# A mixture-of-experts stage whose scatters add straight into the output, with a bound on the row number

## The chip, the cores and the metric

The kernel runs on one core of one Trainium2 chip. TensorE (PE), VectorE (DVE), ScalarE (ACT), GpSimd (POOL) and SyncE (SP) each run their own list of instructions in order and wait for one another on semaphores; 16 DMA engines move data between the core's SBUF and HBM, fed from queues that SP, ACT and POOL issue to. The metric is the device time of one execution in microseconds (us), lower is better. A change is judged by runs of both kernels on the same chip.

## The reference, cut to what matters

One layer over 512 tokens of width 512: cross-attention over 8192 context rows, a Mamba block with an MLP, and a mixture of experts with a shared expert. Each part adds to `x`. The change is in the last part:

```python
logits = jnp.einsum('btc,ec->bte', x, router_w)
top_vals, top_idx = jax.lax.top_k(logits, 2)
gates = jax.nn.sigmoid(top_vals)
w_full = jnp.zeros((N, 16)).at[jnp.arange(N)[:, None], top_idx].add(gates)
gate, up = jnp.split(jnp.einsum('nc,ech->neh', xf, gate_up_w), 2, axis=-1)
out_all = jnp.einsum('neh,ehc->nec', jax.nn.silu(gate) * up, down_w)
moe = jnp.einsum('ne,nec->nc', w_full, out_all)
...
return moe + shared
...
x = x + ffn(layernorm(x), ...)
```

Each of the 512 tokens goes to 2 of 16 experts, so there are 1024 pairs of token and expert. The kernel computes only these. With the inputs of the reference the router sends 27, 19, 24, 112, 116, 16, 61, 45, 28, 72, 36, 46, 53, 165, 142 and 62 tokens to experts 0 to 15.

## The kernel before, in words

The attention takes the first 1.8 ms or so, the Mamba block and its MLP most of the rest, the experts the last 0.18 ms. Only the last part is touched.

**Sorting the tokens.** Tokens are sorted into blocks of 128 slots: blocks 0 to 15 are the experts' own, blocks 16 to 22 take what an expert has above 128. A slot is a row of `xd_d` in HBM: the normed token in two fp16 halves, the number of the row that its result goes to, and its gate. Early in the kernel (`weight_prep`, L512 on) every slot is filled with zeros and the row number 512 + p for partition p, an address behind the 512 tokens. `route` (L1240) then writes the 1024 real slots over it with eight scatters. A block's filled slots are its lowest, since tokens are numbered within their expert; the empty ones keep the row numbers 512 to 639.

**The sum.** `sum_d` (L66) is a scratch tensor in HBM with 512 + 128 rows of 512 fp32 values; the last 128 are the dump for empty slots, zeroed at L524. When the residual `x_sb` with the shared expert's result is ready, POOL copies it to the first 512 rows (L1416). Each block's result is then added to the rows its slots name. At the end SP copies the 512 rows to the output (L1425).

**The experts' loop** is `moe` (L1363). Blocks 0 to 17 always run (`16 + MOV`, MOV = 2); blocks 18 to 22 only where `total`, the number of extra blocks in use, is above 2 (L1421). For each block k:

- SP loads the weights in pieces of 512 KB (`piece`, L1135: `wef`), six of one expert; ACT makes the fp16 high half (L1148), DVE the low half (L1149). Twenty gate/up pieces are ready before the loop starts.
- `moe_load` (L1300) loads block k + 3 into a tile `xd` (6 buffers): the first three from POOL's queue, the others from ACT's.
- TensorE transposes the block's tokens (L1315), ACT copies them out (L1401, `xk`), TensorE multiplies by gate and up (L1328), ACT and DVE do silu and the product (L1336 to L1341), TensorE multiplies the block before by its down weights (L1349).
- `moe_out` (L1355) scales the result by the gate on ACT (L1357, `myo`) and issues the scatter on POOL (L1358): one instruction that adds 128 rows of 2 KB into rows of HBM, given by the list `row`, which lies in the block's `xd` tile.

Two blocks may hold the same token, so a scatter waits until the one before it has landed; the tile framework sets this wait, as it does for every tensor that is written twice. The same framework makes a load into a reused `xd` buffer wait until the scatter that reads the row list in it has landed. ACT issues that load in order with its other work, so ACT waits too.

On POOL's queue in this stage are, in order: the eight scatters of `route`, three loads of `xd`, the copy of L1416 and the 18 scatters. On SP's queue are the weights and, last, the copy of L1425.

Of the kernel before, what the change touches and what calls it, by code (L numbers as in the profile page):

```python
# [9 lines left out]
F32 = mybir.dt.float32  # L10
U16 = mybir.dt.uint16
AF = mybir.ActivationFunctionType
ALU = mybir.AluOpType
# [4 lines left out]
P = 128  # L18
NQ = 512
DM = 512  # L20
# [21 lines left out]
def perceiver_layer(ctx: ExitStack, tc: tile.TileContext, a: dict, out: bass.AP):  # L42
    nc = tc.nc

    const = ctx.enter_context(tc.tile_pool(name="const", bufs=1))
    scr = ctx.enter_context(tc.tile_pool(name="scr", bufs=1, space=DRAM))
# [3 lines left out]
    x_sb = const.tile([P, 4, DM], F32, name="x_sb")  # L50
# [12 lines left out]
        for n, k in (("inp", 8), ("outp", 4), ("w1", 8), ("w3", 8), ("w2", 8), ("rsg", 4), ("rsu", 4), ("rsd", 4), ("Wo", 4))  # L63
    }

    sum_d = scr.tile([NQ + P, DM], F32, name="sum_d")  # L66
    xd_d = scr.tile([(16 + NOV) * P, XR], U16, name="xd_d")

    def norm_stats(pool, src, tag):
# [442 lines left out]
    def weight_prep():  # L512
        zero = sb2.tile([P, 2 * DM], F16, name="zero", tag="t2k", bufs=4)
        nc.gpsimd.memset(zero, 0.0)
        none = sb2.tile([P, 2, 1], mybir.dt.int32, name="none", bufs=1)
        nc.gpsimd.memset(none, 0)
        nc.gpsimd.iota(none[:, 0], pattern=[[0, 1]], base=NQ, channel_multiplier=1)
        for k in range(16 + NOV):
            rows = slice(k * P, (k + 1) * P)
            nc.sync.dma_start(xd_d[rows, 0 : 2 * DM], zero.bitcast(U16))  # L520
            nc.sync.dma_start(xd_d[rows, 2 * DM : XR], none.rearrange("p a o -> p (a o)").bitcast(U16))
            if k % 4 == 3 or k == 15 + NOV:
                yield
        nc.sync.dma_start(sum_d[NQ : NQ + P, :], zero.bitcast(F32))  # L524
        blocks = [(name, i, dst) for name in mlp_d for i, dst in enumerate(mlp_d[name])]

        def fetch(j):
            f = sb2.tile([P, 1024], F32, name="mpf", bufs=2)
            nc.sync.dma_start(f, a[blocks[j][0]][:, blocks[j][1]])
            return f  # L530

        nf = fetch(0)
        yield
        for j, (name, i, dst) in enumerate(blocks):
            f = nf
            if j + 1 < len(blocks):
                nf = fetch(j + 1)
            yield
            for h in range(2):
                sl = slice(h * 512, h * 512 + 512)  # L540
                hl = sb2.tile([P, 2, 512], F16, name="mph", tag="t2k", bufs=4)
                nc.vector.tensor_scalar(hl[:, 0], f[:, sl], WF, None, ALU.mult)
                nc.vector.scalar_tensor_tensor(hl[:, 1], f[:, sl], WF, hl[:, 0], ALU.mult, ALU.subtract)
                nc.sync.dma_start(dst[:, :, sl], hl)
                yield
# [20 lines left out]
    advance(start + LEAD)  # L566
    load(1)
    pend, enders, early = [], [], weight_prep()
    NFILL = 12 * NSTEP - 6
    rate = ((NPASS - 1) * PASSN + LAST - LEAD) / NFILL  # L570
# [44 lines left out]
    for m in range(NSTEP):  # L615
        n = NLAST * NSTEP + m
        if m % 4 == 0:
            load(n // 4 + 1)
        cur = scores(u, m, loads[n // 4], sp, True)
        while len(pend) > 1:  # L620
            drain()
        pend.append((u, m, cur))
        if m == 0:
            tl = tail(tc, a, out, const, scr, ident, x_sb, mlp_d, oT, sum_d, xd_d, (ps_s, ps_o, ps_x, bank_j))
        for _ in range(2):
            if m >= 1 and not ready:
                ready = next(tl)
# [12 lines left out]
def tail(tc, a, out, const, scr, ident, x_sb, mlp_d, oT, sum_d, xd_d, psums):  # L640
    nc = tc.nc
# [493 lines left out]
    def piece(k, t, i):  # L1135
# [23 lines left out]
        out=lt, in_=lt, pattern=[[1, P]], compare_op=ALU.is_gt, fill=0.0, base=0, channel_multiplier=-1  # L1159
# [195 lines left out]
    def moe_out(py, row, gate_):  # L1355
        yo = g2.tile([P, DM], F32, name="myo", tag="yo", bufs=4)
        nc.scalar.activation(yo, py, AF.Copy, scale=gate_)  # L1357
        nc.gpsimd.indirect_dma_start(  # L1358
            out=sum_d[:], out_offset=bass.IndirectOffsetOnAxis(ap=row, axis=0), in_=yo, in_offset=None,
            compute_op=ALU.add,  # L1360
        )

    def moe(ks, ready):  # L1363

        last = ks[-1]
        todo = [(k, i) for k in ks for i in range(4)][ready:]
        each = len(todo) // (len(ks) - 1)
        free = [NWE - ready]  # L1370

        def split(n):
            n = min(n, len(todo), free[0])
            free[0] -= n
            for _ in range(n):
                k, i = todo.pop(0)
                piece(k, "gu", i)
            return n

        lastk[0] = last  # L1380
        for k in range(ks[0], ks[0] + 3):
            moe_load(k, nc.gpsimd)
        piece(ks[0], "dn", 0)
        xin_ = moe_in(ks[0])
        nc.scalar.copy(xin_[0], xin_[1])
        prev, out_ = None, None
        for k in ks:
            if out_:
                moe_out(*out_)
                out_ = None  # L1390
            piece(k, "dn", 1)
            n = split(each)
            xk, _, *to = xin_
            mid = moe_mid(*moe_up(k, xk))
            free[0] += NC4
            if k < last:
                xin_ = moe_in(k + 1)
            next(mid)
            moe_load(k + 3, nc.scalar)
            if k < last:  # L1400
                nc.scalar.copy(xin_[0], xin_[1])  # L1401
            gg = next(mid)
            split(each - n)
            while (k + 1, "gu", 3) not in W and k < last:
                split(1)
            if k < last:
                piece(k + 1, "dn", 0)
            if prev:
                out_ = moe_down(*prev[0:2]), *prev[2]
            prev = k, gg, to  # L1410
        if out_:
            moe_out(*out_)
        moe_out(moe_down(*prev[0:2]), *prev[2])

    regs = [nc.sync.value_load(oii[0:1, k : k + 1], min_val=0, max_val=15) for k in range(NOV)]
    nc.gpsimd.dma_start(sum_d[0:NQ].rearrange("(p i) d -> p i d", i=4), x_sb)  # L1416
    assert next(pre, None) is None
    moe(range(16 + MOV), NWE)
    mo.close()
# [1 line left out]
    with tc.If(total > MOV):  # L1421
        for n in range(4):
            piece(16 + MOV, "gu", n)
        moe(range(16 + MOV, 16 + NOV), 4)
    nc.sync.dma_start(out, sum_d[0:NQ].rearrange("(p i) d -> p i d", i=4))  # L1425
    es.close()


# [66 lines left out]
```

## Time and profile before

| | us |
|---|---|
| median of 3 runs (lowest, highest) | 2570.77 (2567.15, 2572.27) |
| the profiled execution | 2565.43 |
| its span, first to last instruction | 2563.7 |
| TensorE busy in the span | 2361.3 (92%) |
| POOL busy in the span | 73.8 (3%) |
| first scatter of the experts starts at | 2404.55 |
| last scatter of the experts starts at | 2551.43 |
| granted TensorE clock, mean | 0.979 |

The span is cut into 40 slices of 64 us, and each digit is the busy share in tenths. The experts' stage is the last three slices: there the DMA engines are as busy as at any time, and POOL, idle for most of the kernel, has its scatters.

```profile
PE   7999899999999999999999998998878678899896
POOL 3000000000000000000000000000000000001112
DMA  7983777787777787777778664777711212388897
```

The stage by itself, in stretches: busy time of each engine with the number of instructions, then granted clock, share of the 16 DMA engines and GB/s.

```profile
2404.00:2440.00 36.00, 31.63 (x416) 25.11 (x414) 28.58 (x29) 29.07 (x36) 8.85 (x4) 1.00 1.00 348
2440.00:2470.00 30.00, 29.74 (x425) 25.05 (x422) 25.29 (x25) 26.47 (x33) 5.52 (x3) 1.00 1.03 361
2470.00:2500.00 30.00, 28.93 (x375) 22.78 (x373) 24.65 (x25) 23.59 (x29) 4.80 (x3) 1.00 1.03 354
2500.00:2530.00 30.00, 28.17 (x400) 23.76 (x399) 23.37 (x23) 25.98 (x32) 6.49 (x4) 1.00 1.02 364
2530.00:2564.00 34.00, 16.28 (x189) 11.78 (x186) 10.89 (x11) 10.99 (x15) 7.46 (x4) 0.78 0.48 111
```

The columns of engines are PE, PEld (weight load, beside PE), DVE, ACT and POOL. In the middle stretches all but POOL are busy for most of the time and the DMA is full; in the last one the weights have all arrived and little but scatters is left.

### The profile page before, as it was taken

To read this page: it belongs to the slowest core of one execution; us is meant where nothing else is said; L and a number is where in the kernel's file an instruction comes from. 1 tells how busy PE (TensorE), PEld (TensorE's weight loads), DVE (VectorE), ACT (ScalarE), POOL (GpSimd) and SP (SyncE) were. 2 spreads that over 40 slices of the span, in tenths; PEclk is the share of its full clock that TensorE was granted. 3 is DMA by queue.
4 is the path that set the end of the run, shared out by engine and by line. 5 is a ranking of instruction groups with operands and counts; after the bars stand their busy time and mean duration, and the time that the engine had idled before them with its cause. 6 is when DMAs were issued, how large, how long until landed. Compare 5 with 4: busy or idle time off the path is not lost. (4 is left out here: it accounts for less than half of the span.)

```text
span 2563.7 us, 56681 instructions
## 1 busy us (share of the span) xinstructions
PE 2361.3 (92%) x22958; PEld 1722.3 (67%) x22958; DVE 2046.2 (80%) x2378; ACT 1947.5 (76%) x3734; POOL 73.8 (3%) x77
## 2 busy tenths in 40 slices
PE   7999899999999999999999998998878678899896
PEld 3555577777666777766777776897756456577775
DVE  6776578888888888887888777998899999746685
ACT  5787788888878888877888888997958557434685
POOL 3000000000000000000000000000000000001112
PEclk9999999999999999999999999999999889999998
DMA  7983777787777787777778664777711212388897
GB/s 267 304 272 133 215 213 227 231 238 232 216 231 227 219 247 236 226 213 213 240 216 234 175 171 133 196 207 210 200 59 40 101 50 84 125 281 274 315 360 232
DMA packets 355199, 529.52 MB, mean 207 GB/s; under 512 B 28194, under 2 KB 221922, under 8 KB 354660
## 3 DMA queue, kind: packets, MB, share of 16 engines
q1 hardware_dynamic: 349156, 513.23, 65.7%
q0 software_dynamic: 3616, 8.66, 1.5%
q8 instruction: 182, 2.98, 0.5%
q10 hardware_dynamic: 2160, 3.95, 0.5%
q14 instruction: 85, 0.70, 0.1%
HBM read 396.65 MB, written 126.97 MB: 204 GB/s over the span
## 5 line engine op out<-in xcount | busy, mean ns | idle before, releaser
L380 DVE TENSOR_TENSOR phl<-p,phl 128x1024 f16<-128x1024 f32 x512 | 626.8, 1225 | 191.5 <-ACT phl L377 175.6
L375 ACT ACTIVATE p<-pss 128x512 f32<-128x512 f32 x1024 | 597.6, 622 | 112.1 <-issue 43.5
L308 ACT ACTIVATE sf<-psx 128x512 f16<-128x512 f32 x1024 | 558.6, 625 | 70.2 <-PE psx L303 69.5
L367 PE MATMUL pss<-qhh,k 128*128 128x256 f16 x2048 | 478.3, 274 | 14.1 <-ACT phl L377 11.9
L368 PE MATMUL pss<-qlm,kb 128*128 128x256 f16 x2048 | 477.1, 273 | 0.8 <-DMA v<-v_d 0.7
L316 DVE TENSOR_TENSOR runm<-runm,sf 128x2048 f16<-128x2048 f16 x240 | 292.4, 1220 | 51.4 <-ACT sf L308 51.3
L397 PE MATMUL po<-v,phl 128*128 128x130 f16 x4096 | 322.3, 220 | 3.9 <-DVE oq L410 3.4
L377 ACT ACTIVATE phl<-pss 128x512 f16<-128x512 f32 x512 | 312.8, 611 | 0.0
L397 PEld LDWEIGHTS <-phl 128*128 128x128 f16 x4096 | 270.5, 98 | 61.7 <-issue 15.3
L278 PE MATMUL psv<-wh_v,ctxc 128*128 128x256 f16 x1024 | 283.4, 277 | 7.3 <-ACT wh_v L179 3.2
L279 PE MATMUL psv<-wl_v,ctxc 128*128 128x256 f16 x1024 | 282.0, 275 | 1.1 <-DVE wl_v L180 1.1
L280 PE MATMUL psv<-wh_v,ctxc 128*128 128x256 f16 x1024 | 282.0, 275 | 0.0
L367 PEld LDWEIGHTS <-k 128*128 128x128 f16 x2048 | 200.3, 98 | 65.0 <-issue 20.0
L368 PEld LDWEIGHTS <-kb 128*128 128x128 f16 x2048 | 200.7, 98 | 52.1 <-issue 14.9
L303 PE MATMUL psx<-khl,qh 64*128 64x512 f16 x1024 | 208.1, 386 | 18.2 <-ACT sf L308 13.1
L929 PE MATMUL py<-hs,ident 128*128 128x256 f32 x512 | 141.2, 430 | 76.6 <-DVE hs L926 76.5
L400 PE MATMUL po<-v,phl 128*128 128x65 f16 x4096 | 208.2, 193 | 1.4 <-DVE phl L380 1.4
L254 PE MATMUL psk<-ctxc,wh_k 128*128 128x512 f16 x512 | 197.4, 386 | 10.8 <-ACT ctxc L237 9.0
L379 DVE CAST phl<-p 128x1024 f16<-128x1024 f32 x256 | 176.1, 688 | 30.8 <-ACT p L375 30.6
L255 PE MATMUL psk<-ctxc,wh_k 128*128 128x512 f16 x512 | 196.0, 383 | 0.9 <-DVE ctxc L238 0.9
L256 PE MATMUL psk<-ctxc,wl_k 128*128 128x512 f16 x512 | 195.9, 383 | 0.0
L929 PEld LDWEIGHTS py<-hs,ident 128*128 128x128 f32 x512 | 104.8, 213 | 108.3 <-DVE hs L926 90.9
(315 smaller groups left out, 3814.4 us busy)
## 6 DMA issues: line engine op xcount, KB each, us to landing
v<-v_d SPq DMA_DIRECT2D x128, 520.0 KB
k<-k_d SPq DMA_DIRECT2D x256, 256.0 KB
ctxc<-ctx_d SPq DMA_DIRECT2D x96, 512.0 KB
wef<-in_gu_dram SPq DMA_DIRECT2D x72, 512.0 KB
v_d<-vs SPq DMA_DIRECT2D x128, 260.0 KB
k_d<-khl SPq DMA_DIRECT2D x128, 256.0 KB
kb<-k_d SPq DMA_DIRECT2D x128, 256.0 KB
wpm<-w_d SPq DMA_DIRECT2D x48, 512.0 KB
```

The costliest lines, as they stand in the source:

```text
L278: nc.tensor.matmul(ps[:, t, :], lhsT=ct[i // 2][:, 0, i % 2, sl], rhs=wh[:, i, :], start=i == 0, stop=False)
L279: nc.tensor.matmul(ps[:, t, :], lhsT=ct[i // 2][:, 0, i % 2, sl], rhs=wl[:, i, :], start=False, stop=False)
L280: nc.tensor.matmul(ps[:, t, :], lhsT=ct[i // 2][:, 1, i % 2, sl], rhs=wh[:, i, :], start=False, stop=i == NC4 - 1)
L308: nc.scalar.activation(dst, ps, AF.Copy, scale=1.0 / (8.0 * WS))
L316: nc.vector.tensor_tensor(r, r, sf, ALU.max)
L367: nc.tensor.matmul(ps[:, hh], lhsT=k[:, hh, sl], rhs=qhh[:, hh, qs], start=True, stop=False)
L368: nc.tensor.matmul(ps[:, hh], lhsT=b[:, hh, sl], rhs=qlm[:, hh, qs], start=False, stop=True)
L375: nc.scalar.activation(p32[:, i], pss[i], AF.Exp, scale=sc)
L377: nc.scalar.activation(ph[:, i], pss[i], AF.Exp, scale=sc)
L380: nc.vector.tensor_tensor(pl, p32, ph, ALU.subtract)
L397: nc.tensor.matmul(o, lhsT=ph[:, i, hh, qs], rhs=vv, start=first, stop=False, **kw)
L929: nc.tensor.matmul(py[:, j, :], lhsT=ident, rhs=hs[:, n, 1:], start=k == 0, stop=False)
```

## The change

The scratch tensor `sum_d` goes; its name now stands for the output, seen as 512 rows. The zeroing of its dump rows goes, and the copy at the end. The scatter gets a bound, `NQ - 1` = 511, with `oob_is_err=False`: a row number above it is no error, and its row is left out. The slots' row numbers are as before, so an empty slot still says 512 + p.

```diff
-    sum_d = scr.tile([NQ + P, DM], F32, name="sum_d")
+    sum_d = out.rearrange("p i d -> (p i) d")
...
-        nc.sync.dma_start(sum_d[NQ : NQ + P, :], zero.bitcast(F32))
...
         nc.gpsimd.indirect_dma_start(
-            out=sum_d[:], out_offset=bass.IndirectOffsetOnAxis(ap=row, axis=0), in_=yo, in_offset=None,
-            compute_op=ALU.add,
+            out=sum_d, out_offset=bass.IndirectOffsetOnAxis(ap=row, axis=0), in_=yo, in_offset=None,
+            bounds_check=NQ - 1, oob_is_err=False, compute_op=ALU.add,
         )
...
-    nc.gpsimd.dma_start(sum_d[0:NQ].rearrange("(p i) d -> p i d", i=4), x_sb)
+    nc.gpsimd.dma_start(out, x_sb)
...
-    nc.sync.dma_start(out, sum_d[0:NQ].rearrange("(p i) d -> p i d", i=4))
```

The row number of a token is 4p + i for partition p and column i of `x_sb`, in the scratch tensor as in the output, so the numbers that the slots carry stay right.

## The prediction

> **What bounds the kernel now.** I read the chain that ended last first, then the scatters in order of time, then one stretch of the timeline with every engine, then the DMA queues of that stretch, and last the waits at the end.
>
> ```profile
> 2545.94 1.55 DMA sum_d<-myo,xd
> 2547.49 3.74 issue
> 2551.22 0.49 POOLq L1420
> 2551.72 1.26 POOL sum_d L1358
> ```
>
> The chain ends in scatters (L1358): one lands, the next goes out. The whole list of scatters shows how far back this reaches. Scatter 0 starts at 2404.55, scatter 17 at 2551.43: 17 gaps, 8.64 us each on average. The tile view gives the landing (start to last byte) as 4.8 least, 8.0 median, 10.2 most.
>
> ```profile
> 2472.88 1.55 POOL L1358 DMA_INDIRECT sum_d<-myo,xd  x1 [7.26 <-issue]
> 2475.00 0.68 ACT L1357 ACTIVATE myo<-acc,xd 128x512 f32<-128x512 f32 x1
> ...
> 2481.62 0.33 ACTq L1300 DMA_DIRECT2D xd<-xd_d  x1
> 2481.99 1.01 ACT L1401 COPY xk<-pxd 128x1024 f16<-128x1024 f16 x1 [2.04 <-DMA sum_d<-myo,xd]
> 2482.26 1.55 POOL L1358 DMA_INDIRECT sum_d<-myo,xd  x1 [7.83 <-issue]
> ```
>
> Columns: start, duration, engine and line; in brackets the idle time before. The next `myo` is ready at 2475.68, yet its scatter starts at 2482.26: it waits for the scatter of 2472.88, whose rows it may share. ACT waits for the same landing at L1300, because the new `xd` takes the buffer (one of 6) whose row list that scatter still reads. From that release to the next scatter's start 0.64 us pass (2481.62 to 2482.26; the same at 2463.43, 2489.74, 2499.91, 2507.89 and 2517.34). So a gap is landing + 0.64, and 17 x (8.0 + 0.64) = 146.9, exactly the 146.88 from first to last: every gap is set by a landing. `myo` is ahead of its scatter by 0.28 us at scatter 0, 7.1 at scatter 10, 4.4 at scatter 17.
>
> TensorE is close behind. Its cycle per expert, from transposes to transposes (L1315), is 8.39 where nothing waits (2426.45 to 2434.84, 2444.30 to 2452.69). Over the 14 cycles from 2405.38 to 2532.54 the excess over 8.39 is 127.16 - 117.46 = 9.7 us; the five cycles in which L1300 came late (2463 to 2527) hold 3.8 of it, weights most of the rest. And the DMA engines are full (2463 to 2475):
>
> ```profile
> q1 hardware_dynamic: 1078, 3.92, 83.9%
> q0 software_dynamic: 144, 0.26, 12.0%
> ```
>
> q0 is a single scatter: 144 packets, which I read as 128 rows and 16 completions, 0.26 MB and 12% of 16 engines. Alone, without weights beside it, a scatter lands in 4.8.
>
> The end, by SP's and POOL's own waits:
>
> ```profile
> 2551.43 1.55 POOL L1358 DMA_INDIRECT sum_d<-myo,xd  x1 [3.94 <-issue]
> 2557.31 0.59 SPq L1425 DMA_DIRECT2D out_dram<-sum_d  x1
> ...
> SPq L1425 <- DMA sum_d<-myo,xd: 20.1, 1, 20.1
> SPq L1490 <- DMA out_dram<-sum_d: 4.2, 1, 4.2
> ...
> L1490 POOLq DRAIN  x1: 2520/2520/2520, 2557.3 to 2557.3; - x1
> ```
>
> POOL's last wait for scatter 17 ends at 2556.4, SP is let go at 2557.25, the copy of 1 MB is issued and lands by 2562.4, the closing barrier ends at 2563.7.
>
> **The end copy, removed.** SP stood still for nothing else, and nothing is queued behind it. Without it SP would be at its closing waits at 2557.3, but POOL's drain runs from 2557.3 to 2559.8, and the barrier needs it. If the drain stays, 2562.4 - 2559.8 = 2.6 us are saved; if it was held up by the copy, 2562.4 - 2557.3 = 5.1. I take 2.6: the copy is SP's, not POOL's.
>
> **Edits at nothing.** The zeroing of the dump rows (L524) is one 256 KB issue of 0.45 us on SP at 293.9; SP's next issue is at 303.5 and TensorE, VectorE and ScalarE are at 0.7 to 0.9 there; uncovered it would be 0.45. L1416 writes the same 1 MB from the same queue to another tensor; issued at 2379.91, landed in 5.9, it is over 18 us before scatter 0. The order among copy and scatters now hangs on the output tensor; I take it to be kept, wait for wait, with the same things queued behind (POOL has only scatters; ACT's stall at L1300 as before).
>
> **The bound: what it costs.** No row shows a scatter with a bound. The check is POOL work for 128 rows. The plain scatter L1240 takes 0.96 us at least, the adding one 1.54: one more duty on each row costs 0.58. The slowest adding scatter took 2.63, 1.1 more than the fastest. So 0 to +1.1 a scatter; I take +0.2, a third of the 0.58, as a bare comparison sends no second transfer.
>
> **The bound: what it saves.** 18 blocks of 128 slots are 2304 rows, of which 512 x 2 = 1024 are filled: 1280 rows (56%) are dropped, 2 KB read, added and written each. Lower bound: nothing, if each dropped row still makes a transfer or the slowest engine keeps its rows. Upper bound: a plain load of 257 KB (`xd<-xd_d`) lands in 3.9 in the same traffic, so at most 8.0 - 3.9 = 4.1 of a landing belongs to the rows, and 56% is 2.3. I take 1.0, under half, because filled slots are the low partitions and need not leave all engines alike. Net landing: -0.8 (bounds -2.3 and +1.1). At the end, without traffic, the rows' part is at most 4.8 - 3.4 (the quickest `xd` load) = 1.4; the last two blocks hold 37 and 14 rows by the router, so -1.0 and -1.25, +0.2 each.
>
> The Trainium skill, "DMA: Bandwidth & Descriptors", section "Anatomy of one DMA — SWDGE (gpsimd) path", fits 2.0 us plus bytes over 436 GB/s: 2.6 for this scatter, where the trace has 4.8 alone and 8.0 in traffic, and 0.33 for the dropped bytes. With -0.33 in place of -0.8 I estimate a total of -7.7, or 2563.
>
> **The sum, on the profiled span of 2563.7.** With -0.8 a gap is 7.2 + 0.64 = 7.84, below TensorE's 8.39, so the lead of `myo` runs out and TensorE decides. It gets back the waits on L1300, 3.8; I take 3, since the weights (ScalarE waited 5.6 us for them) take some. The last three `myo` end at 2535.5, 2541.4, 2544.0 in place of 2538.5, 2544.4, 2547.0. Scatter 15 starts at 2535.8 (+0.28) and lands in 5.3 - 0.7 = 4.6 at 2540.4; scatter 16 starts at 2541.7 and lands in 4.0 at 2545.7; scatter 17 at 2546.3 and lands in 3.8 at 2550.1, in place of 2556.4: -6.3. With the copy -2.6: -8.9, span 2554.8. The profiled execution took 2565.43, the median of the runs is 2570.77; I carry the difference over: 2570.8 - 8.9 = 2561.9, so **2562**.
>
> **Rivals.** *Landings stay as long.* Filled slots lie on the low partitions; 128 rows on 16 engines are 8 each, and if an engine owns a group of neighbouring partitions, a half-filled block leaves the low engines their 8 rows and only idles the others. For it: the landing counts the slowest engine. Against: 12% of the DMA time is the scatters', and the engines are full. Then only the copy is won, -2.6 (to -5.1): 2568. The Trainium skill, same page, section "The descriptor swizzle", states such a grouping for a 128-partition transfer, four partitions and the four 32 further on; by it a block of 36 rows or more keeps a full engine. No run here shows the grouping.
>
> *The check is dear.* Scatter 17's traffic begins at 2553.2 by the DMA's slices, after POOL's instruction has ended at 2552.98, so POOL's time adds to the landing in full, and landings set all 17 gaps. At +1.1 and nothing saved, 17 x 1.1 = 18.7; a loop 13% longer thins the weights' traffic, and of the 3.2 us between 8.0 and 4.8 some 0.4 come back: 17 x 0.7 = 11.9, less 2.6: +9.3, **2580**. It decides from a net 2.6 / 17 = 0.15 us a scatter. For it: every gap is bound, and a gain is capped by TensorE while a loss is not. Against: more than half the rows go.
>
> *The order is lost.* If the output is not guarded as `sum_d` was, scatters go as soon as `myo` is there and may lose sums: some 2560, and wrong values.
>
> **Chances.** Forecast 0.47 (own range 2557 to 2566), landings as long 0.20, dear check 0.30, order lost 0.03. About 0.2%, 5.1 us, is what a measurement tells from no change. Faster by more: 0.45 of the forecast, 0.02 of the second, 0.03 of the last, 0.50. Slower by more: 0.28, nearly all of the dear check. Within: 0.22. The range goes from 2554 (all 9.7 us of TensorE's excess, and the drain gone) to 2582, which leaves out the worse half of the dear check.
>
> **What would show it.** L1425 gone and SP's last wait on scatter 17; POOL's drain still 2.5 us. L1358's duration against 1.54 is the check. Landings against 8.0, and q0's packets per scatter below 144, are the rows. If scatters start 0.3 us after `myo` late in the loop, TensorE decides; if `myo` still leads by 4 to 7 us, landings do. I am wrong if L1358 grows by over 0.2 us while landings do not shrink, or if the end waits for something the copy hid.

## The result, and the profile after

| | before | changed |
|---|---|---|
| median of 7 runs, us | 2570.77 | 2561.42 |
| lowest, highest | 2566.87, 2577.71 | 2558.31, 2563.57 |
| ratio (95% interval) | | 0.9961 (0.9951 to 0.9972) |
| span of the profiled execution | 2563.7 | 2558.0 |
| first transposes of the experts start | 2381.06 | 2383.56 |
| last `myo` ends | 2547.01 | 2546.48 |
| first scatter starts | 2404.55 | 2408.52 |
| last scatter starts | 2551.43 | 2550.27 |
| POOL's last wait for it ends | 2556.45 | 2553.85 |

The kernel is faster by 9.4 us. The table splits the spans. From the first transposes to the last `myo` it is 165.95 and 162.92 us: -3.0. From there to the last scatter (the lead) 4.42 and 3.79: -0.6. The last landing, 5.02 and 3.58: -1.4. What follows it, 7.25 and 4.15: -3.1. Together -8.2. The spans differ by 5.7 only, because the experts' stage began 2.5 us later in this execution, with nothing changed ahead of it but one small transfer.

The chain that ended last, in order of time (start, length, what): it still runs from scatter to scatter and ends, as before, with the last one; neither of the two views has a step of SP in it.

```profile
2545.28 1.55 DMA out_dram<-myo,xd
2546.83 3.24 issue
2550.06 0.49 POOLq L1419
2550.56 1.26 POOL out_dram L1357
```

The end: the last scatter; SP's last long wait is on it (the number behind the name is the total wait in us, then how often, then the longest); and POOL's drain has stayed.

```profile
2550.27 1.55 POOL L1357 DMA_INDIRECT out_dram<-myo,xd  x1 [3.44 <-issue]
...
SPq L1488 <- DMA out_dram<-myo,xd: 18.1, 1, 18.1
...
L1488 POOLq DRAIN  x1: 2520/2520/2520, 2554.7 to 2554.7; - x1
```

The same stretch of the loop in the timeline (L1357 is the scatter, L1356 `myo`, L1299 the load of `xd`, L1400 the copy `xk`):

```profile
2474.16 0.33 ACTq L1299 DMA_DIRECT2D xd<-xd_d  x1
...
2474.52 1.01 ACT L1400 COPY xk<-pxd 128x1024 f16<-128x1024 f16 x1 [1.20 <-DMA out_dram<-myo,xd]
...
2474.82 1.55 POOL L1357 DMA_INDIRECT out_dram<-myo,xd  x1 [7.20 <-issue]
...
2476.91 0.68 ACT L1356 ACTIVATE myo<-acc,xd 128x512 f32<-128x512 f32 x1
...
2482.83 0.33 ACTq L1299 DMA_DIRECT2D xd<-xd_d  x1
...
2483.50 1.55 POOL L1357 DMA_INDIRECT out_dram<-myo,xd  x1 [7.12 <-issue]
```

`myo` is ready at 2477.59 and its scatter starts at 2483.50: a lead of 5.9 us, where it was 6.6 at the same block before. ACT still waits for a landing ahead of L1400, 4.4 us in all in place of 6.3. The lead is 2.0 at block 3, 5.8 at block 7, 6.0 at block 10, 5.6 at block 14. Every scatter after the first still goes out on a landing, not on its `myo`.

The scatter itself, by line: on POOL there is one instruction more, a MOVE, which takes 29 ns; the adding scatter takes 1542 ns at least, as before.

```profile
L1357 POOLq MOVE  x18: 29/29/29, 2382.6 to 2545.1; - x18
...
L1357 POOL DMA_INDIRECT out_dram<-myo,xd x18: 1542/1604/2595, 2408.5 to 2550.3; - x18
```

And the queue q0 over the whole kernel, before and then after (packets, MB, share of the 16 engines):

```profile
q0 software_dynamic: 3616, 8.66, 1.5%
```

```profile
q0 software_dynamic: 3616, 6.05, 0.9%
```

The bytes fell by 2.61 MB, which is 1280 dropped rows of 2048 bytes. The packets did not fall at all. The page's count of packets under 512 bytes rose from 28194 to 29442, by 1248, and by 1281 with the bound alone (`e1` below): a dropped row still goes out as a packet, but with hardly anything in it.

### The profile page after: what moved, and what is told of

The parts are those of the page before. It is cut to its first block, busy times and chain, and to the rows that moved or that the text cites. A ratio compares the mean times of both kernels' runs of the same rounds, so it can differ in the third digit from the quotient of the medians.

```text
span 2558.0 us, 56696 instructions
## 1 busy us (share of the span) xinstructions
PE 2372.8 (93%) x22958; PEld 1730.8 (68%) x22958; DVE 2046.4 (80%) x2378; ACT 1947.0 (76%) x3734; POOL 71.9 (3%) x77
## 2 busy tenths in 40 slices
DMA packets 355023, 525.60 MB, mean 205 GB/s; under 512 B 29442, under 2 KB 223170, under 8 KB 354500
## 3 DMA queue, kind: packets, MB, share of 16 engines
q0 software_dynamic: 3616, 6.05, 0.9%
## 5 line engine op out<-in xcount | busy, mean ns | idle before, releaser
L928 PE MATMUL py<-hs,ident 128*128 128x256 f32 x512 | 148.4, 447 | 66.8 <-DVE hs L925 66.7
L254 PE MATMUL psk<-ctxc,wh_k 128*128 128x512 f16 x512 | 197.3, 385 | 10.2 <-ACT ctxc L237 8.4
L928 PEld LDWEIGHTS py<-hs,ident 128*128 128x128 f32 x512 | 110.0, 223 | 101.3 <-DVE hs L925 80.4
```

What stands on the lines that cost most here:

```text
L928: nc.tensor.matmul(py[:, j, :], lhsT=ident, rhs=hs[:, n, 1:], start=k == 0, stop=False)
```

## The experiments

All ratios are to the kernel before, with 95% intervals; a median in us is given beside them. 0.1% is 2.6 us. "Landing" is from a scatter's start to its last byte. To compare landings beside the weights' traffic, I read the tile view of `myo` for 2412 to 2524 us, which holds 11 to 13 of the 18 scatters; for up to three of them the view gives no landing.

**One part at a time.** The bound alone, with scratch sum, dump rows and end copy as before (`e1_bound_only`):

```diff
 # to the kernel before
-            compute_op=ALU.add,
+            bounds_check=NQ - 1, oob_is_err=False, compute_op=ALU.add,
```

> The scratch sum, its dump rows and the copy at the end stay; only the scatters get the bound of 511, so the 1280 empty rows are left out. Shares theory: the copy was worth about 3 of the 9.4 us, shorter landings the other 6, so this runs 5 to 7 us below before (about 2564.5), with the scatters' gaps at some 8.3 us as in the changed kernel. Copy theory: the dropped rows keep their packets and the loop gains nothing beyond chance; only the last two, nearly empty blocks land sooner, 1 to 2 us below before (about 2569).

Measured: 2567.73 us, ratio 0.9985 (0.9974 to 0.9995), -3.9 us (-1.3 to -6.7). This lies between the two expectations; its interval excludes neither. In its profile the chain of 17 gaps is 143.1 us, 3.8 shorter than before, and the last landing 3.6 in place of 4.8.

The end copy alone (`e2_no_end_copy`), and the same with a check that drops nothing (`e4_bound_drops_none`):

```diff
 # to the kernel before: e2, and e4 with the last line too
+        nc.sync.dma_start(out, x_sb)
...
-    nc.sync.dma_start(out, sum_d[0:NQ].rearrange("(p i) d -> p i d", i=4))
...
-            compute_op=ALU.add,
+            bounds_check=NQ + P - 1, oob_is_err=False, compute_op=ALU.add,
```

> No bound; all 128 rows of every block go to the scratch sum with its dump rows. The copy at the end is left out, and the output is written once, early in the kernel, with the first x: the output lacks the sums. Shares theory: only the copy is won, POOL's drain of 2.5 us stays, 3 us below before (about 2568). Copy theory: 7 to 8 us below before (about 2563).

> As the run without the end copy, plus a bound of 639 on the scatters, above every row number: the check is made and nothing is dropped (the output lacks the sums as there). If the check is free on POOL (a MOVE of 29 ns, the scatter's instruction still 1.54 us at least), within 2 us of the run without the end copy. If it delays each landing by 0.15 us or more, 17 gaps make that 2.5 us or more above it.

Measured: 2567.01 us, 0.9984 (0.9973 to 0.9995), -4.1 us; and with the check 2567.49 us, 0.9987 (0.9974 to 1.0), -3.3. The copy theory's 7 to 8 us is outside the first interval (-1.3 to -6.9). From the last scatter's start to the end of the span there are 9.23 and 9.21 us, before 12.27: 3.0 is what the copy costs by the profile. The check costs nothing that can be measured: the two runs agree, and their chains are 147.9 and 147.5. So the two parts of the change are worth about 4 us each; together they make 8, and the whole change, 10.0 by its ratio, is within their intervals.

**How much of a landing are the rows?** Nearly everything dropped (`e3_drop_all`), and half of the rows never sent (`e6_half_rows`):

```diff
 # to the changed kernel: e3
-            bounds_check=NQ - 1, oob_is_err=False, compute_op=ALU.add,
+            bounds_check=0, oob_is_err=False, compute_op=ALU.add,
 # to the changed kernel: e6
-            out=sum_d, out_offset=bass.IndirectOffsetOnAxis(ap=row, axis=0), in_=yo, in_offset=None,
+            out=sum_d, out_offset=bass.IndirectOffsetOnAxis(ap=row[0:64], axis=0), in_=yo[0:64], in_offset=None,
```

> The changed kernel with a bound of 0: all rows but row 0 are left out of the output, so almost nothing is added. If a landing in traffic is set by the bytes of its rows, landings fall from 7.7 to about 6 and TensorE's cycle of 8.4 sets the loop: 3 to 6 us below the changed kernel (about 2557). If it is set by the number of packets (144 a scatter, dropped or not), landings stay above 7 beside the weights and fall only after the weights have ended (5.0 to about 3.5): 1 to 3 us below the changed kernel (about 2559.5).

> The changed kernel, but each scatter takes partitions 0 to 63 only: the rows of slots 64 to 127 are left out (blocks 3, 4, 9, 13 and 14 lose real rows). 64 rows and their completions in place of 144 packets. Packets theory: landings beside the weights fall clearly, from 7.7 to 6 or less, the gaps no longer set the loop, and the time is 3 to 6 us below the changed kernel (about 2557). If neither packets nor bytes but a fixed latency beside the weights sets a landing, landings stay at 7.5 and the time within 2 us of the changed kernel.

Measured: 2555.74 us, 0.9943 (0.993 to 0.9957), and 2557.71 us, 0.9951 (0.9937 to 0.9964). Landings between 2412 and 2524, for the kernel before, for the changed kernel, for all dropped, and for half of the rows:

```profile
DMA to landing us min/median/max: 7.3/8.5/10.2
```

```profile
DMA to landing us min/median/max: 7.1/8.0/9.4
```

```profile
DMA to landing us min/median/max: 5.2/5.8/7.7
```

```profile
DMA to landing us min/median/max: 4.7/5.9/7.5
```

With 144 packets a scatter in both, the changed kernel's landings are 8.0 with 57 real rows on average and those of `e3` 5.8 with next to none: the packets alone do not make the landing. In both experiments the lead of `myo` is 0.3 us at nearly every block from 2 to 16, and the chain is 137.4 and 138.0 us. This is the state that the prediction had expected of the change: TensorE's 8.4 us cycle sets the gaps (8.4 at 11 of the 12 gaps from block 2 to block 14 in the run of half the rows).

**Is it the chain?** Every second block adds to a second sum, so that a scatter waits for the one two before it (`e8_two_sums`), and a buffer of `xd` more, which takes the landing away from ACT but leaves the chain (`e7_xd7`):

```diff
 # to the changed kernel: e8
+    sum_b = scr.tile([NQ, DM], F32, name="sum_b")
+    nout = [0]
...
+        for r in range(4):
+            nc.sync.dma_start(sum_b[r * P : (r + 1) * P, :], zero.bitcast(F32))
...
+        nout[0] += 1
         nc.gpsimd.indirect_dma_start(
-            out=sum_d, out_offset=...
+            out=sum_d if nout[0] % 2 else sum_b[:], out_offset=...
 # to the changed kernel: e7
-        xds[k] = g2.tile([P, XR], U16, name="xd", bufs=6)
+        xds[k] = g2.tile([P, XR], U16, name="xd", bufs=7)
```

> The changed kernel with two sums: every second block adds to the output, the others to a zeroed scratch tensor that is never added, so the output lacks their part. A scatter then waits for the one two before it. If the chain of landings sets the loop's pace and the end, myo's lead falls to about 0.3 us nearly everywhere, the waits of ScalarE on L1299 go, scatter 17 goes out 0.3 us after its myo, and the time falls by 6 to 9 us below the changed kernel (about 2553.5). If TensorE and the weights set the pace and the landings only follow, just the 3.8 us of the last lead go: about 2557.5.

> The changed kernel with 7 in place of 6 buffers for xd: ScalarE's load waits for the landing of one scatter earlier, some 8.5 us more room, so a late landing no longer holds ScalarE and TensorE in the loop. The scatters stay in one chain. If the chain itself sets the end, the time stays within 2 us of the changed kernel, with no wait of L1400 on a scatter and a greater lead of myo at the end. If the harm is through ScalarE's wait, 2 to 4 us below the changed kernel (about 2558.5).

Measured: two sums 2556.65 us, 0.9946 (0.9932 to 0.9959), 4.8 below the changed kernel's median (3.9 by the two ratios, whose intervals overlap; the two were measured on different chips); seven buffers 2562.83 us, 0.9964 (0.9951 to 0.9978), no better than the changed kernel. The time of the two sums is that of the second expectation: little but the last lead is gone. The lead is 0.3 at all 18 blocks, ACT has no wait on a landing, and the last scatters no longer queue up:

```profile
2538.42 2.02 POOL L1363 DMA_INDIRECT sum_b<-myo,xd  x1 [7.51 <-ACT myo L1361]
2543.95 1.55 POOL L1363 DMA_INDIRECT out_dram<-myo,xd  x1 [3.51 <-ACT myo L1361]
2546.54 1.55 POOL L1363 DMA_INDIRECT sum_b<-myo,xd  x1 [1.04 <-ACT myo L1361]
```

In each line the idle time before the scatter now ends with ACT's `myo`, not with a landing. But TensorE hardly gains in the loop: its transposes of blocks 3 and 17 lie 121.7 us apart here and 122.7 in the changed kernel. With seven buffers ACT's wait on landings was gone, too, and yet the lead was 6.2 at block 10 and 4.2 at block 17: the lead at the end belongs to POOL's chain, and ACT's wait costs the changed kernel next to nothing.

**Which rows, and when.** In the two-sums kernel every scatter goes out 0.3 us after its `myo`, whatever its landing, so landings can be compared at one point of the loop. Nothing dropped (`e9_two_sums_none_dropped`: both sums in scratch with dump rows, the output written early as in `e2`), and filled slots spread over the partitions (`e10_two_sums_spread`, and `e5_spread_slots` with one sum):

```diff
 # to the changed kernel: e5; in e10 with the two sums of e8
         nc.vector.tensor_copy(sg, sf_)
...
+        nc.vector.tensor_scalar(sga, sg, 31, 2, ALU.bitwise_and, ALU.logical_shift_left)
+        nc.vector.tensor_scalar(sgb, sg, 5, 3, ALU.logical_shift_right, ALU.bitwise_and)
+        nc.vector.tensor_tensor(sga, sga, sgb, ALU.bitwise_or)
+        nc.vector.tensor_scalar(sgb, sg, 7, 7, ALU.logical_shift_right, ALU.logical_shift_left)
+        nc.vector.tensor_tensor(sg, sga, sgb, ALU.bitwise_or)
 # to e8: e9
-            bounds_check=NQ - 1, oob_is_err=False, compute_op=ALU.add,
+            compute_op=ALU.add,
```

> Two sums in turn, both in scratch with dump rows, no bound: all 128 rows of each block move, and every scatter goes out 0.3 us after its myo. The output gets only the first x. If dropping rows shortens a landing at the same point of the loop, the landings beside the weights (blocks 0 to 12) are longer than the 7.2 us (median) of the two sums with the bound: 8 or more. If the landing depends only on when in the loop a scatter goes out, they are 7.2 too.

> Two sums in turn with the bound, and a block's slots spread over the partitions as in the spread run; the second sum is never added. All scatters go out 0.3 us after their myo, so landings compare at the same point of the loop. If the fullest engine's rows set a landing, the median beside the weights falls from 7.2 to 6.5 or less. If only the total of bytes or packets counts, it stays at 7.2. Time within 2 us of the two sums with low slots (2556.65) either way, as nothing waits for a landing.

> The changed kernel with the slot number's low seven bits turned round (slot s of a block goes to partition 4 (s mod 32) + s div 32), five small VectorE instructions more before the first scatter: a block's filled rows lie over all partitions in place of the low ones. If the fullest DMA engine sets a landing, the half-filled blocks land sooner, by 0.5 us or more each, and the kernel is 2 to 5 us below the changed one (about 2558). If the number of packets sets it, landings and time stay within 2 us of the changed kernel, the five instructions costing up to 1 us.

Measured: nothing dropped 2559.9 us, 0.9954 (0.9938 to 0.997); spread with two sums 2562.02 us, 0.9956 (0.9939 to 0.9973); spread with one sum 2559.43 us, 0.9955 (0.9942 to 0.9969). The landings between 2412 and 2524 with two sums, for nothing dropped, for the empty rows dropped, and for the same with spread slots:

```profile
DMA to landing us min/median/max: 7.3/7.9/9.1
```

```profile
DMA to landing us min/median/max: 5.9/7.3/8.4
```

```profile
DMA to landing us min/median/max: 6.7/7.4/8.3
```

Dropping the empty rows takes 0.6 us off a landing; spreading the rest takes off nothing. So beside the weights it is not the fullest engine's rows that count. The packets do count for something: `e6` and `e8` both keep a lead of 0.3, and in the seven blocks that lose no real row in `e6` and whose landing both profiles give (1, 2, 5, 6, 7, 10 and 11) the median is 5.9 us with 64 slots sent and 7.2 with 128. Not sending 64 empty slots is worth 1.3 us there; dropping the bytes of all empty slots, with their packets kept, 0.6. At the end, where no weights move, spreading does help: blocks 15, 16 and 17 land in 4.8, 4.2 and 3.3 us in the changed kernel and in 4.0, 3.5 and 3.2 with one sum and spread slots. That is too little: the spread kernel's ratio is not to be told apart from the changed kernel's 0.9961. The median of the two-sums spread run is 5 us above the 2556.65 of its twin with low slots, against an expectation of 2, but the two ran on different chips, the ratios' intervals overlap, and in its profile the experts' stage began at 2393.3.

The distance between the transposes of blocks 3 and 17, read from the timeline of each profile, sorts the kernels (14 cycles; at 8.39 us each they would take 117.5):

| rows of the empty slots | one chain | two sums |
|---|---|---|
| moved | 127.2 (before), 128.1 (`e2`), 127.8 (`e4`) | 123.5 (`e9`) |
| dropped | 122.7 (changed), 123.9 (`e1`), 122.5 (`e7`), 123.6 (`e5`) | 121.7 (`e8`), 122.2 (`e10`), 121.0 (`e11`) |
| all rows dropped | 120.7 (`e3`) | |
| half of the slots not sent, empty rows dropped | 121.1 (`e6`) | |

With all rows moved the chained loops take 3.7 to 4.6 us longer than the unchained one, with the empty rows dropped 0.3 to 2.9. The bound takes 3 to 6 us out of a chained loop, by seven profiles, and 1.3 to 2.5 out of an unchained one, where ACT's wait for gate and up weights goes from 8.0 (`e9`) to between 3.3 and 5.1 us (`e8`, `e10`, `e11`). So read, the bound works in two ways, on the chain and on the weights; no run takes the second by itself. The new target of the scatters adds little of its own in the loop: `e1`, which drops the same rows and adds into the scratch tensor, takes 123.9, within 1.4 us of the three chained kernels that add into the output.

A last reading sets the same rows in the two kinds of kernel side by side. With the empty rows dropped the median landing is 7.3 to 7.4 us in the three kernels with two sums, at a lead of 0.3, and 7.9 to 8.5 in the four with the chain (8.0 in the changed one). With all rows moved it is 7.9 (`e9`) and 8.5 to 9.0 (before, `e2`, `e4`). So landings are longer by 0.5 us or more where scatters wait in the chain. Going out late does not explain that by itself: in the changed kernel those before 2470 land in 8.5 and those after it, at the greatest leads, in 7.8, where the two-sums kernel (`e8`) has 7.3 and 7.7. Nor does it follow from the nearness of ACT's load of 257 KB (L1299). That load starts within 1.5 us of the scatter in the changed kernel from block 2 on, and about 3 to 4 us after it in `e8`. But with seven buffers (`e7`) it starts 1.6 to 3.2 us ahead of the scatter after 2470, and the landings there are 7.7, much as the changed kernel's 7.8.

**Could the chain be bought off?** The two sums with spread slots, joined at the end (`e11_two_sums_joined`), and a shorter queue of weights (`e12_wef4`):

```diff
 # to e10: e11
+    nc.gpsimd.dma_start(out, sum_b[:].rearrange("(p i) d -> p i d", i=4), accum_op=ALU.add, max_dma_last_dim=512)
 # to the changed kernel: e12
-        f = g2.tile([P, 1024], F32, name="wef", bufs=6)
+        f = g2.tile([P, 1024], F32, name="wef", bufs=4)
```

> As the run before, and at the end POOL adds the second sum (1 MB) into the output with one adding transfer: the whole result. If that transfer lands in about 6 us without other traffic, the gain of the two sums (4.8 us below the changed kernel) is spent: 2561 to 2564. If it lands in 3 to 4, it is 2 us below the changed kernel (about 2559.5).

> The changed kernel with 4 in place of 6 buffers for the arriving weights, so SP keeps at most 4 transfers of 512 KB on the way. If the landings beside the weights are long because of the depth of the weights' queue, they fall from 8.1 (mean of blocks 1 to 12) to 7.4 or less, the lead of myo runs out and the time falls 3 to 6 us below the changed kernel (about 2557). If the weights' bytes in all and not their depth matter, landings stay at 8 and the weights come later: ScalarE's waits for wef grow from 3.5 us and the time rises by 2 to 15 us.

Measured: joined 2569.38 us, 0.9991 (0.9981 to 1.0001); four buffers 2591.73 us, 1.0067 (1.005 to 1.0084). Both lose. SP's waits of the joined kernel show why:

```profile
SPq L1502 <- DMA out_dram<-sum_b: 11.0, 1, 11.0
```

The adding transfer of 1 MB lands in 10.3 us, not in 6: the row of the plain 1 MB copy was no guide to an adding one. With four buffers a part of each half of the expectation came true: landings fall to 7.5 and the lead runs out, but ACT waits 28.2 us for gate and up weights in place of 3.5, and the time rises by 30 us over the changed kernel's median, where 15 were the most expected:

```profile
ACT we L1147 <- DMA wef<-in_gu_dram: 28.2, 34, 2.0
```

No version tried beats the changed kernel by more than its interval with the whole result.

## Why the prediction was right, point by point

The total was right, 2562 against 2561.42. By the profiles the sum was -8.9 forecast and -8.2 found beside the late start of the stage. One step of it failed, and TensorE's share came by another way than was said, so that the total fits so closely is in part luck.

- **The end copy.** -2.6 was forecast, with POOL's drain staying on the path; the drain is there unchanged (2520 ns) and the part after the last landing fell by 3.1, by 3.0 in `e2`. The 0.5 beyond the forecast lies in the closing barrier: it ended 1.3 us after the copy landed, and ends 0.8 after the drain now.
- **Edits at nothing.** The order was kept: scatters still wait for one another on the output, with the same wait in front of each. That excludes the rival of the lost order.
- **The check.** +0.2 us a scatter was taken; a MOVE of 29 ns is all that was found, and `e4` agrees. The rival of the dear check, the one with 0.30, falls with that; what a scatter that lands later would have cost was not tried.
- **The rows' saving.** -1.0, and -0.8 net, was forecast for a landing beside the weights. At the same point of the loop it is -0.6 (`e9` against `e8`), in the chain itself -0.5 (8.5 to 8.0). The upper bound it was taken from rested on a row from another place: the loads of 257 KB that landed in 3.9 were POOL's, at 2378 ahead of the loop, and ACT's of the same size in the changed kernel's loop land in 6.3 to 7.7 us, so by that row less of a landing is the rows' than the 4.1 allowed. The sign named for the rows, fewer than 144 packets a scatter, did not show: only the bytes went. The rival "landings stay as long" was half right: they did fall, but by little. Its mechanism, the fullest engine, is not seen beside the weights (spread against low slots: 7.4 in `e10` against 7.3 in `e8`, 7.9 in `e5` against 8.0) and shows only in the last blocks. There the forecast of 4.0 for block 16 stands against 4.2.
- **TensorE's gain.** 3 of the 3.8 us of waits on L1300 were forecast for the last `myo`; it came 3.0 earlier, measured from the stage's start. The number fits by luck, for those waits are not what went: ACT still waits 4.4 of the 6.3 us for landings, and in `e7`, which has none of these waits, the loop is no shorter (122.5 against 122.7). From block 3 to block 17 the loop won 4.5 us. A part of that are ACT's waits for gate and up weights, 3.5 us in place of 5.6, in which the prediction saw no gain. Ahead of block 3 the stage took 1.5 longer (25.8 against 24.3), as it does in several runs with nothing changed there. Without the chain (`e8`) the loop is 1.0 shorter still.
- **The failed step: "the lead of `myo` runs out and TensorE decides".** TensorE does decide, nearly, but the lead did not run out. A gap was to be 7.84, below the cycle of 8.39, and both parts of that were mis-sized. The 8.64 it started from is the mean of all 17 gaps, and the last three, 5.5 to 6.0 us with no weights beside them, pull it down. The 13 gaps from scatter 1 to scatter 14 were 9.11 each before, with a median landing of 8.5, not 8.0; less the 0.8 forecast that is 8.31, hardly below 8.39. And what came off was 0.3, to 8.83, where the `myo` of these blocks follow one another at 8.56, so nothing draws the lead down. At scatter 17 it is 3.8 us, 2.3 were forecast, and 4.4 were there before: 1.5 us of the sum did not come. The mis-sized term is the landing. At a lead of 0.3 it is 7.3, and a gap of 7.94 would have been enough. But the first landing takes 10.2 us before and 10.1 in the changed kernel and puts the scatters behind, the next ones let the lead grow to 5.8 by block 7, and there it stays. A slow first landing is not needed for that: in `e5` it is 7.4, the lead is 0.3 up to block 3, and still 4.8 at block 14. `e3`, `e6` and `e8` show the loop without a lead, 4 to 6 us further down by the medians, 3 to 5 by the ratios.
- **The last landing.** 3.75 us with 14 rows, 1.2 less than before, was forecast: 3.3 by the tile view, 3.58 to POOL's release, -1.4.
- **The share from the Trainium skill**, "DMA: Bandwidth & Descriptors", section "Anatomy of one DMA — SWDGE (gpsimd) path": 0.33 us for the dropped bytes was under the 0.5 to 0.6 measured, and its 2.6 for the whole scatter is far below the 4.7 at least that a scatter with all 128 rows moved took.
- **The grouping by partitions** that the same page's section "The descriptor swizzle" states: by it spreading takes a block of 62 rows from eight rows on the fullest engine to four, and without traffic such a block does land 0.8 us sooner. The trace agrees so far; beside the weights the rule decides nothing.

Open is why landings are longer where scatters wait in the chain. That they are is seen in seven profiles against four with two sums; neither the lead nor the nearness of the `xd` load is shown to be the cause.

## What to carry to other kernels

Where transfers must wait for one another, compare landing plus restart with the cycle of the busiest engine, and take both over the same stretch: a mean over the whole chain took in the quick transfers of the end and made a gap look half a microsecond shorter than it was beside the weights. A chain that has fallen behind stays behind unless its gap is clearly the shorter. Leaving rows out of a scatter saves their bytes and not their packets: 56% of the rows gave 6 to 8% of a landing, and in the loop without the chain 1.3 to 2.5 us, with shorter waits for the weights, which share the DMA engines. Not sending a slot at all was worth more than dropping its row. A second accumulator takes the chain apart at once, but price the joining transfer as an adding one before building it.

## What the hardware showed that was not expected

- A row that the bound drops is still a packet: 3616 on the queue with and without the bound, and with nearly all rows dropped; only bytes fall (8.66, 6.05 and 3.97 MB).
- One adding transfer of 1 MB between two tensors in HBM landed in 10.3 us with no other traffic, where SP's plain copy of the same 1 MB landed 5.1 us after its issue began (2557.31 to 2562.4).
- The time at which the experts' stage began varied between 2381.1 and 2387.3 us over the profiles of kernels with almost the same code ahead of it. A comparison of two single profiles cannot settle 4 us; the gaps inside the stage can.
